# Two attention layers in fp32: where the reciprocals are issued, where the bias is added, and when the left factors are made

## The chip, the cores and the metric

The kernel runs on one core of a Trainium2 chip. A core has five engines that run side by side, each in its own order: TensorE (PE in the profile; PEld is its weight load), VectorE (DVE), ScalarE (ACT), GpSimd (POOL) and SyncE (SP), which here issues the transfers. The metric is the time of the core on the device in microseconds, as the median of three runs; lower is better.

## The reference, cut to what matters

Two attention blocks follow each other on eight images of 512 channels and 32 x 32 = 1024 tokens, all in fp32. The second has the same computation with 32 groups instead of 8.

```python
# x: (8, 512, 32, 32); C = 512, 8 heads of 64, N = 1024
xn = group_norm(x) * gn_scale + gn_bias            # 8 groups, then 32
q, k, v = split(einsum('oc,bcn->bon', qkv_w, xn) + qkv_b)
attn = softmax(einsum('bhdi,bhdj->bhij', q, k) / 8)
out = einsum('bhij,bhdj->bhdi', attn, v)
x = einsum('oc,bcn->bon', proj_w, out) + proj_b + x
```

## The kernel before

A unit is one layer of one image; there are 16, numbered from 0. Each runs through Q, K, V, the projection of the unit before it, and then attention. Products of 512 x 512 with 512 x 1024 are done by a scheme of seven half-size products with sums of factors (Winograd's form of Strassen's), and in Q, K and the projection some of the seven are cut into seven once more ("inner products"). So sums of left factors (weights) and right factors (activations) have to be made, and sums of results behind the products. In Q and K the order of the seven products is 1, 6, 2, 7, 5, 4, 3; those of INNER = (2, 5, 4, 3) are inner ones from unit 1 on.

```python
# pools (cut): ppool holds 4 tiles (exp tiles p, residual x, u3 of the first unit), accpool 2,
# trpool 2, tmppool 1, rbpool 1, tpool 1 of each tag, wpool 1 of each tag

    def blocks(name, left, right, tokens, c11, others, done, u3, inner=None, rests=None,
               rests_in=None):
        # bx, by, bz, sbank[1]: the four pairs of PSUM banks
        bx, by, bz = apair[0], sbank[0], apair[1]
        sums, taken = [], []
        ... # products(bank, k, start, stop): factor k of seven, added into bank
        def inner_products(bank, k, one, two, first=False):
            # a product cut once more into seven of half the size; three quarters end in
            # bank, the rest is copied by ScalarE into the tile "rest"
            ...
            product(1, one, True, False)
            nc.scalar.copy(rest[:, 0, :FD2], one)
            product(2, bank[:, 0, :FD2], first, True)
            product(3, bank[:, 0, FD2:], False, True)
            product(6, one, False, False)
            nc.scalar.copy(rest[:, 0, FD2:], one)
            product(5, two, True, True)
            nc.scalar.copy(rest[:, 1, FD2:], two)
            product(4, bank[:, 1, :FD2], first, True)
            product(7, one, False, True)
            taken.append(nc.scalar.copy(rest[:, 1, :FD2], one))
            return rest
        def add_rest(r, h, rest):
            if rest is not None:
                add = nc.gpsimd.tensor_add
                add(rest[:, 0, FD2:], rest[:, 0, FD2:], rest[:, 1, FD2:])
                add(rest[:, 1, FD2:], rest[:, 1, :FD2], rest[:, 1, FD2:])
                rests(r, h, rest)

        ...
        products(bx, 1, True, False)
        p1 = work(accpool, "acc", "p1")
        nc.scalar.copy(p1, bx)
        done(sums)
        products(by, 6, True, False)
        u2 = work(trpool, "tr", "u2")
        nc.vector.tensor_add(u2, by, p1)
        done(sums)
        rest = inner_products(bx, 2, sbank[1], bz)
        c11(bx)
        add_rest(0, 0, rest)
        done(sums)
        products(by, 7, False, False)
        if isinstance(u3, tuple):
            u3 = work(*u3, "u3")
        else:
            sums.append(u3)
        nc.vector.tensor_add(u3, by, p1)
        done(sums)
        twice = inner_products(bz, 5, sbank[1], bx, True)
        others(1, 1, bz, u3, twice)
        add_rest(1, 1, twice)
        done(sums)
        rest = inner_products(by, 4, bx, sbank[1])
        others(1, 0, by, p1)
        add_rest(1, 0, rest)
        done(sums)
        rest = inner_products(bz, 3, sbank[1], bx)
        others(0, 1, bz, u2, twice)
        add_rest(0, 1, rest)
        if twice is not None:
            rests(0, 1, twice)
        done(sums)
        return taken[-1:]
    def projections(w, rest):
        ...
        # done(_) counts the products of Q, K and V from 1 to 21 and runs the parts in rest[count]
        for sel, bias in (("q", QB), ("k", KB)):
            ...
            def others(r, h, bank, more, part=None):
                for i in range(2):
                    pr = 2 * r + i
                    n = FD if part is None or i == 0 else FD2
                    w.last[sel].append(
                        nc.vector.scalar_tensor_tensor(
                            tiles[pr][:, h * FD : h * FD + n], bank[:, i, :n],
                            vec[:, l, bias, pr : pr + 1], more[:, i, :n], ALU.add, ALU.add,
                        )
                    )
                if part is not None:
                    w.last[sel].append(
                        nc.scalar.activation(
                            tiles[pr][:, h * FD + FD2 : (h + 1) * FD], more[:, 1, FD2:],
                            AF.Identity, bias=vec[:, l, bias, pr : pr + 1],
                        )
                    )
            def rests(r, h, rest):
                for i in range(2):
                    cols = tiles[2 * r + i][:, ts(h, FD)]
                    w.last[sel].append(nc.gpsimd.tensor_add(cols, cols, rest[:, i, :]))

            ...
    # the projection behind attention: same blocks(); its results are stored by SyncE
    # inside attention
        def reciprocals(pr):
            def work(name):
                return small.tile([BL, 2 * BL], F32, tag=name, name=f"{name}_{u}_{pr}", bufs=1)
            lt = state["lt"]
            one, two, tot, rows, rec = map(work, ("one", "two", "tot", "rows", "rec"))
            nc.vector.tensor_add(
                one, state["red"][:BL].rearrange("i j h f -> i (j h f)"), lt[:, 0, :]
            )
            nc.vector.tensor_add(two, lt[:, 1, :], lt[:, 2, :])
            nc.vector.tensor_add(tot, one, two)
            nc.vector.transpose(rows, tot)
            nc.vector.reciprocal(rec, rows)
            ok = okay[:BL]
            nc.vector.scalar_tensor_tensor(ok, tot, SUM_MAX, ok, ALU.is_le, ALU.mult)
            nc.vector.scalar_tensor_tensor(ok, tot, SUM_MIN, ok, ALU.is_ge, ALU.mult)
            drec = dram.tile([2, N], F32, tag="drec", name=f"drec_{u}_{pr}")
            ... # rec goes to DRAM and back as rb, spread over the partitions, for divide(pr)
        ...
        parts = {4: [lambda: reciprocals(CC - 1)], 10: [divide_last], 17: mixing[:2], 18: mixing[2:3],
                 19: mixing[3:]}
    # left factors of the inner products, made once in each layer
    def mix_inner_left(l, lefts, ks, dst):
        sub = nc.gpsimd.tensor_sub
        def part(n, i, after):
            left = lefts[i][ks[n]]
            t = tpool.tile([P, 2, FD], F32, tag=("o1", "o2", "o4")[n % 3], name=f"l{i}{n}_{l}")
            s1, s2, s4 = (t[:, 0, j * P : (j + 1) * P] for j in range(3))
            a11, a12 = left[:, 0, :P], left[:, 1, :P]
            a21, a22 = left[:, 0, P:], left[:, 1, P:]
            first = nc.gpsimd.tensor_add(s1, a21, a22)
            first = getattr(first, "ins", first)
            tc.add_manual_dep(first, name_of(after), DEP, reason="spread over attention")
            sub(s2, s1, a11)
            sub(a21, a11, a21)
            sub(s4, a12, s2)
            nc.sync.dma_start(dst[l][:, i, n], t[:, 0, : 3 * P].rearrange("p (s o) -> p s o", s=3))
        return [partial(part, n, i) for n in range(len(ks)) for i in range(len(lefts))]

    # main loop over 16 units (2 layers x 8 images), cut
        left_parts = []
        if u == 0:
            left_parts = mix_inner_left(0, lefts[:2], INNER, inner_left)
        elif u == B - 1:
            left_v, mixing_w = mix_weights(1, load_weights(1, (2,)), nc.vector, 2)
            lefts = coming[0] + left_v
            left_parts = [lambda _, i=i: [part() for part in mixing_w[i : i + 2]] for i in (0, 2)]
            left_parts += mix_inner_left(1, lefts[:2], INNER, inner_left)
        elif u in (1, B + 1):
            left_parts = mix_inner_left(units[u][0], [left_o], INNER_O, inner_left_o)
            # in a step of attention (8 chunks of 8 steps):
            if left_parts and t in (3, 7) and s >= (3 + late) * NT - 1:
                left_parts.pop(0)(state["exp"][-1])
```

Of the kernel before, what the change touches and what calls it, by code (L numbers as in the profile page):

```python
# [11 lines left out]
F32 = mybir.dt.float32  # L12
# [6 lines left out]
P = 128  # L19
# [13 lines left out]
def fast_path(ctx, tc, x, qkv_wT, proj_wT, vecs, groups, out, flag):  # L33
# [184 lines left out]
    def mix_inner_left(l, lefts, ks, dst):  # L218


        sub = nc.gpsimd.tensor_sub

        def part(n, i, after):
            left = lefts[i][ks[n]]
            t = tpool.tile([P, 2, FD], F32, tag=("o1", "o2", "o4")[n % 3], name=f"l{i}{n}_{l}")
            s1, s2, s4 = (t[:, 0, j * P : (j + 1) * P] for j in range(3))
            a11, a12 = left[:, 0, :P], left[:, 1, :P]
            a21, a22 = left[:, 0, P:], left[:, 1, P:]
            first = nc.gpsimd.tensor_add(s1, a21, a22)
            first = getattr(first, "ins", first)  # L230
            tc.add_manual_dep(first, name_of(after), DEP, reason="spread over attention")
            sub(s2, s1, a11)
            sub(a21, a11, a21)
            sub(s4, a12, s2)
            nc.sync.dma_start(dst[l][:, i, n], t[:, 0, : 3 * P].rearrange("p (s o) -> p s o", s=3))

        return [partial(part, n, i) for n in range(len(ks)) for i in range(len(lefts))]

# [116 lines left out]
    def blocks(name, left, right, tokens, c11, others, done, u3, inner=None, rests=None,  # L355
               rests_in=None):
# [53 lines left out]
        def add_rest(r, h, rest):  # L410
            if rest is not None:
                add = nc.gpsimd.tensor_add
                add(rest[:, 0, FD2:], rest[:, 0, FD2:], rest[:, 1, FD2:])
                add(rest[:, 1, FD2:], rest[:, 1, :FD2], rest[:, 1, FD2:])
                rests(r, h, rest)
# [11 lines left out]
        nc.vector.tensor_add(u2, by, p1)  # L427
# [10 lines left out]
        nc.vector.tensor_add(u3, by, p1)  # L438
# [3 lines left out]
        add_rest(1, 1, twice)  # L442
# [7 lines left out]
        add_rest(0, 1, rest)  # L450
# [3 lines left out]
        return taken[-1:]  # L454

    def projections(w, rest):
# [13 lines left out]
        for sel, bias in (("q", QB), ("k", KB)):  # L470
# [12 lines left out]

            def others(r, h, bank, more, part=None):

                for i in range(2):
                    pr = 2 * r + i
                    n = FD if part is None or i == 0 else FD2
                    w.last[sel].append(
                        nc.vector.scalar_tensor_tensor(  # L490
                            tiles[pr][:, h * FD : h * FD + n], bank[:, i, :n],
                            vec[:, l, bias, pr : pr + 1], more[:, i, :n], ALU.add, ALU.add,
                        )
                    )
                if part is not None:
                    w.last[sel].append(
                        nc.scalar.activation(
                            tiles[pr][:, h * FD + FD2 : (h + 1) * FD], more[:, 1, FD2:],
                            AF.Identity, bias=vec[:, l, bias, pr : pr + 1],
                        )  # L500
                    )

            def rests(r, h, rest):
                for i in range(2):
                    cols = tiles[2 * r + i][:, ts(h, FD)]
                    w.last[sel].append(nc.gpsimd.tensor_add(cols, cols, rest[:, i, :]))  # L506
# [3 lines left out]
            if w.inner:  # L510
# [5 lines left out]
                f"{sel}_{u}", left, w.right, False, c11, others, done, u3, inner, rests,  # L516
                {
# [21 lines left out]
        blocks(f"v_{u}", w.lefts[2], w.right, True, v11, v_others, done, (ppool, "p"))  # L539

    def project(w, after):
# [47 lines left out]
        def rests(r, h, rest):  # L589
            for i in range(2):  # L590
                o = 2 * r + i
                cols = results[o, h]
                nc.gpsimd.tensor_add(cols, cols, rest[:, i, :])
                store(o, h)
# [3 lines left out]
            f"o_{w.u}", w.left, w.right_o, False, c11, others, done, (rbpool, "rb"), w.inner_o, rests,  # L598
# [29 lines left out]
    def attention(w, at_step, at_end):  # L628
# [193 lines left out]
        parts = {4: [lambda: reciprocals(CC - 1)], 10: [divide_last], 17: mixing[:2], 18: mixing[2:3],  # L822
# [51 lines left out]
    for u in range(2 * B):  # L874
# [14 lines left out]
        if u == B - 1:  # L889
# [8 lines left out]
            for i in range(2):  # L898
                rest.setdefault(20 + i, []).append(partial(mix_coming, i))
        projections(w, rest)  # L900
# [13 lines left out]
        if u == 0:  # L914
            left_parts = mix_inner_left(0, lefts[:2], INNER, inner_left)
        elif u == B - 1:
            left_v, mixing_w = mix_weights(1, load_weights(1, (2,)), nc.vector, 2)
            lefts = coming[0] + left_v
            left_parts = [lambda _, i=i: [part() for part in mixing_w[i : i + 2]] for i in (0, 2)]
            left_parts += mix_inner_left(1, lefts[:2], INNER, inner_left)  # L920
        elif u in (1, B + 1):
            left_parts = mix_inner_left(units[u][0], [left_o], INNER_O, inner_left_o)
# [5 lines left out]
        if old is not None:  # L928
# [4 lines left out]
            project(old, lambda g: stats_of(*stats_after.get(g, ())))  # L933
# [53 lines left out]
    project_last(old, [part for g in (4, 10) for part in rest[g]] + [verdict])  # L987
# [265 lines left out]
```

## Time and profile before

| | |
|---|---|
| time, median of 3 | 3295.59 us (3292.41 to 3295.63) |
| span of the profiled run | 3293.9 us, TensorE clock 0.999 |
| one unit, from Q's first product to the next unit's | about 203 us (409.0 to 612.2) |
| ... of it Q, K, V and the projection | about 93 us (409.0 to 501.9) |
| POOL's adds of 128x512 in Q, L506 | 150, mean 1366 ns |
| VectorE's sum of exp tiles, L708 | 768, mean 1259 ns |

The profile is one execution recorded by the hardware. Its page gives the busy time of each engine, the chain of work that ended last, and groups of equal instructions by source line. The trace behind it answers closer questions: the list of waits says which engine stood before which line, for whom, how long in total and how often; the timeline lists instructions in order of time. In a line such as "PE L393 MATMUL s<-xn,s4w 128*128 128x256 f32 x2" the parts are engine, source line, operation, tile written and tiles read, shape, and how many records are merged. An idle time ahead of an instruction stands in square brackets with the one that ended it.

### The profile page before, as it was taken

What the parts mean: (1) busy time and instruction counts of PE and PEld (TensorE: products, weight loads), DVE (VectorE), ACT (ScalarE), POOL (GpSimd) and SP (SyncE); (2) the same over time, 40 slices, a digit from 0 to 9 for tenths busy, and PEclk for the clock granted to TensorE, in tenths of its full rate; (3) what the DMA queues carried; (4) which work ended last, traced back from release to release, by engine and by line L of the source; (5) the groups of instructions that cost most, each with busy time, mean ns of one, the idle gap of its engine ahead of it and who ended that gap; (6) DMA issues with size and microseconds to landing.
All of it is one profiled execution on the core that took longest, in us unless ns stands there. A gap on an engine that the chain in (4) does not pass through costs nothing.

```text
span 3293.9 us, 55690 instructions
## 1 busy us (share of the span) xinstructions
PE 3259.4 (99%) x21956; PEld 1805.8 (55%) x21956; DVE 2465.0 (75%) x2989; ACT 1648.3 (50%) x2245; POOL 1208.4 (37%) x1200
## 2 busy tenths in 40 slices
PE   8999999999999999999999999999999999999999
PEld 4455474554746547465474645646556464464643
DVE  4876958769586795868958679586795967859577
ACT  1552726536265462744637436374463735637354
POOL 0171171541716317062570603706226072350710
PEclk9999999999999999999999999999999999999999
DMA  2112120121201212022121111201212012120121
GB/s 79 39 60 72 33 84 30 46 78 41 78 28 40 78 41 84 21 66 91 60 84 34 53 61 46 91 15 40 84 42 84 15 40 84 47 78 15 60 77 48
DMA packets 78105, 185.17 MB, mean 56 GB/s; under 512 B 22032, under 2 KB 26768, under 8 KB 77840
## 3 DMA queue, kind: packets, MB, share of 16 engines
q1 hardware_dynamic: 77840, 181.54, 16.2%
q8 instruction: 178, 2.92, 0.4%
q14 instruction: 87, 0.71, 0.1%
HBM read 141.52 MB, written 38.40 MB: 55 GB/s over the span
## 4 chain that ended last, share of the span: by engine, by line
PE 95%; DVE 4%; issue 1%; DMA 0%; ACT 0%; POOL 0%; SPq 0%; DVEq 0%; ACTq 0%
PE a L689 26%; PE s L661 25%; PE s L375 15%; PE a L375 14%; PE a L393 7%; PE s L393 5%; PE a L661 1%; DVE two L751 1%; DVE tot L752 1%; DVE q L490 0%; PE s L609 0%; PE a L609 0%; DVE acc L708 0%; DVE one L748 0%; DVE okay L757 0%
## 5 line engine op out<-in xcount | busy, mean ns | idle before, releaser
L669 ACT ACTIVATE p<-s 128x1024 f32<-128x1024 f32 x976 | 997.0, 1023 | 563.3 <-PE s L661 528.2
L689 PE MATMUL a<-p,v 64*64 64x512 f32 x8192 | 1097.2, 590 | 2.7 <-ACT p L669 2.5
L661 PE MATMUL s<-q,k 64*64 64x512 f32 x7808 | 1055.2, 590 | 1.4 <-DVE v L534 1.4
L708 DVE TENSOR_TENSOR acc<-acc,p 128x1024 f32<-128x1024 f32 x768 | 966.9, 1259 | 75.2 <-ACT p L669 21.6
L689 PEld LDWEIGHTS a<-p,v 64*64 64x64 f32 x8192 | 379.0, 131 | 503.5 <-ACT p L669 354.5
L661 PEld LDWEIGHTS s<-q,k 64*64 64x64 f32 x7808 | 376.6, 133 | 441.5 <-issue 432.9
L884 POOL TENSOR_TENSOR r<-xn 128x256 f32<-128x256 f32 x30 | 51.6, 1720 | 993.2 <-DVE acc L708 813.2
L300 POOL TENSOR_TENSOR y<-var,half 128x4 f32<-128x4 f32 x16 | 31.2, 1949 | 500.2 <-DVE var L298 500.2
L506 POOL TENSOR_TENSOR q<-q,m_q 128x512 f32<-128x512 f32 x150 | 201.1, 1366 | 0.0
L506 POOL TENSOR_TENSOR k<-k,m_k 128x512 f32<-128x512 f32 x150 | 186.6, 1270 | 0.0
L706 DVE TENSOR_TENSOR acc<-p,p 128x1024 f32<-128x1024 f32 x128 | 156.2, 1220 | 18.9 <-ACT p L669 18.9
L721 DVE STREAM_TRANSPOSE tr<-acc 128x1024 f32<-128x1024 f32 x128 | 157.9, 1233 | 0.0
L731 DVE TENSOR_REDUCE red<-tr 128x32 f32<-128x1024 f32 x128 | 153.9, 1202 | 0.6
L715 DVE TENSOR_TENSOR ao<-a,tmp 128x512 f32<-128x512 f32 x128 | 87.9, 687 | 65.8 <-ACT tmp L714 65.8
L423 ACT COPY p_o<-a 128x1024 f32<-128x1024 f32 x15 | 15.2, 1012 | 242.6 <-PE a L375 242.6
L375 PE MATMUL a<-xn,w 128*128 128x512 f32 x272 | 125.9, 606 | 4.0 <-DVE xn L328 4.0
L375 PE MATMUL s<-xn,w 128*128 128x512 f32 x256 | 115.2, 592 | 1.7 <-DVE xn L172 1.7
L375 PE MATMUL a<-w,xn 128*128 128x256 f32 x512 | 115.7, 379 | 0.0
L375 PE MATMUL s<-x_t,s2w 128*128 128x512 f32 x256 | 115.1, 592 | 0.0
L375 PEld LDWEIGHTS a<-w,xn 128*128 128x128 f32 x512 | 97.3, 190 | 13.7 <-issue 0.5
L771 DVE SCALAR_TENSOR_TENSOR ao<-ao,rb 128x1024 f32<-128x1024 f32 x64 | 99.6, 1556 | 6.4 <-DMA rb<-drec 6.3
L322 ACT ACTIVATE xn<-xn,shift,scale 128x512 f32<-128x512 f32 x124 | 99.4, 804 | 6.7 <-DVE shift L318 6.7
(269 smaller groups left out, 4551.5 us busy)
## 6 DMA issues: line engine op xcount, KB each, us to landing
rb<-drec SPq DMA_DIRECT2D x128, 256.0 KB, 3.9
il<-il SPq DMA_DIRECT2D x30, 768.0 KB, 5.3
xn<-mid SPq DMA_DIRECT2D x36, 512.0 KB, 7.5
xn<-x_dram SPq DMA_DIRECT2D x32, 512.0 KB, 6.9
x<-x_dram SPq DMA_DIRECT2D x32, 512.0 KB, 4.7
x<-mid SPq DMA_DIRECT2D x28, 512.0 KB, 4.7
mid<-u_o SPq DMA_DIRECT2D x32, 256.0 KB, 2.0
out_dram<-u_o SPq DMA_DIRECT2D x28, 256.0 KB, 2.1
```

Source lines behind the costliest of these rows:

```text
L322: nc.scalar.activation(cols, cols, AF.Identity, bias=st["shift"][:, c : c + 1], scale=st["scale"][:, c : c + 1],)
L375: nc.tensor.matmul(dst, at[:, c, ts(i, P)], moving[:, c, :], start=start and c == 0 and not (tokens and i % 2), stop=stop and c == 1, skip ...
L393: nc.tensor.matmul(dst, left[j], right[j], start=start, stop=stop, skip_group_check=True)
L506: w.last[sel].append(nc.gpsimd.tensor_add(cols, cols, rest[:, i, :]))
L661: nc.tensor.matmul(bank[e * H : (e + 1) * H, j, :], w.k[pr][j * H : (j + 1) * H, t * P + e * H : t * P + (e + 1) * H], w.q[pr][j * H : (j ...
L669: exp = nc.scalar.activation(p, bank, AF.Exp, scale=SCALE)
L689: nc.tensor.matmul(banks[r][j * H : (j + 1) * H, :], w.v[rows, t, lo : lo + D], p[rows, j, :], start=(t == 0), stop=(t == NT - 1),)
L706: nc.vector.tensor_add(acc, state["first"], p)
L708: nc.vector.tensor_add(acc, acc, p)
L721: nc.vector.transpose(tr, state["acc"].pop(c))
L731: nc.vector.tensor_reduce(red[:, :, qh, :], state["tr"].rearrange("p j (f i) -> p j f i", i=BL), AX.X, ALU.add)
L771: nc.vector.scalar_tensor_tensor(w.ao[pr // 2][:, pr % 2, :], w.ao[pr // 2][:, pr % 2, :], 1.0, state["rb"], ALU.mult, ALU.mult, accum_out ...
```

## The change

It has three parts. (Hunks that only pass an argument on are left out of the diff.) The reciprocals of the last pair of heads of the unit before (seven small operations of VectorE behind a transfer, for the softmax's division) are issued behind the third product of Q, not behind the fourth. The bias of Q and K is added where the two sums u2 and u3 are built, for the right half of the tokens, so that the take of the result is a plain add there and ScalarE's separate bias pass over a quarter tile (which an inner product leaves unwritten in PSUM) isn't needed; GpSimd adds the rest to the sum directly. And the sums of left factors for the inner products, which GpSimd makes once for each layer and spread over an attention stage, are made in V's stage of the first unit for layer 0, and in the projection's stage of unit 7 for layer 1, in buffers that are free there: V's weights' buffers in unit 7, for which V's own new weights are loaded later.

```diff
--- before.py
+++ after.py
@@ -220,21 +220,26 @@
 
         sub = nc.gpsimd.tensor_sub
 
-        def part(n, i, after):
+        def part(n, i, room, after=None):
             left = lefts[i][ks[n]]
-            t = tpool.tile([P, 2, FD], F32, tag=("o1", "o2", "o4")[n % 3], name=f"l{i}{n}_{l}")
-            s1, s2, s4 = (t[:, 0, j * P : (j + 1) * P] for j in range(3))
+            s1, s2, s4 = (room[:, j * P : (j + 1) * P] for j in range(3))
             a11, a12 = left[:, 0, :P], left[:, 1, :P]
             a21, a22 = left[:, 0, P:], left[:, 1, P:]
             first = nc.gpsimd.tensor_add(s1, a21, a22)
             first = getattr(first, "ins", first)
-            tc.add_manual_dep(first, name_of(after), DEP, reason="spread over attention")
+            if after is not None:
+                tc.add_manual_dep(first, name_of(after), DEP, reason="spread over attention")
             sub(s2, s1, a11)
             sub(a21, a11, a21)
             sub(s4, a12, s2)
-            nc.sync.dma_start(dst[l][:, i, n], t[:, 0, : 3 * P].rearrange("p (s o) -> p s o", s=3))
+            nc.sync.dma_start(dst[l][:, i, n], room.rearrange("p (s o) -> p s o", s=3))
 
         return [partial(part, n, i) for n in range(len(ks)) for i in range(len(lefts))]
+
+    def left_rooms(name, pool, tag, cols):
+
+        t = pool.tile([P, cols], F32, tag=tag, name=name)
+        return [t[:, i : i + 3 * P] for i in range(0, cols - 3 * P + 1, 3 * P)]
 
     def load_inner_left(u):
 
@@ -407,12 +412,13 @@
... (add_rest takes alone=None and hands it on to rests)
@@ -424,7 +430,7 @@
         done(sums)
         products(by, 6, True, False)
         u2 = work(trpool, "tr", "u2")
-        nc.vector.tensor_add(u2, by, p1)
+        summed(0, u2, by, p1)
         done(sums)
         rest = inner_products(bx, 2, sbank[1], bz)
         c11(bx)
@@ -435,11 +441,11 @@
             u3 = work(*u3, "u3")
         else:
             sums.append(u3)
-        nc.vector.tensor_add(u3, by, p1)
+        summed(1, u3, by, p1)
         done(sums)
         twice = inner_products(bz, 5, sbank[1], bx, True)
         others(1, 1, bz, u3, twice)
-        add_rest(1, 1, twice)
+        add_rest(1, 1, twice, u3)
         done(sums)
         rest = inner_products(by, 4, bx, sbank[1])
         others(1, 0, by, p1)
@@ -447,11 +453,14 @@
         done(sums)
         rest = inner_products(bz, 3, sbank[1], bx)
         others(0, 1, bz, u2, twice)
-        add_rest(0, 1, rest)
+        add_rest(0, 1, rest, u2 if twice is not None else None)
         if twice is not None:
             rests(0, 1, twice)
         done(sums)
         return taken[-1:]
+
+    def plain_sum(_, to, bank, more):
+        nc.vector.tensor_add(to, bank, more)
 
     def projections(w, rest):
 
@@ -481,29 +490,36 @@
                         )
                     )
 
+            def summed(r, to, bank, more):
+                for i in range(2):
+                    pr = 2 * r + i
+                    nc.vector.scalar_tensor_tensor(
+                        to[:, i, :], bank[:, i, :], vec[:, l, bias, pr : pr + 1], more[:, i, :],
+                        ALU.add, ALU.add,
+                    )
+
             def others(r, h, bank, more, part=None):
 
                 for i in range(2):
                     pr = 2 * r + i
                     n = FD if part is None or i == 0 else FD2
+                    to, one, two = tiles[pr][:, h * FD : h * FD + n], bank[:, i, :n], more[:, i, :n]
                     w.last[sel].append(
+                        nc.vector.tensor_add(to, one, two) if h else
                         nc.vector.scalar_tensor_tensor(
-                            tiles[pr][:, h * FD : h * FD + n], bank[:, i, :n],
-                            vec[:, l, bias, pr : pr + 1], more[:, i, :n], ALU.add, ALU.add,
+                            to, one, vec[:, l, bias, pr : pr + 1], two, ALU.add, ALU.add
                         )
                     )
-                if part is not None:
-                    w.last[sel].append(
-                        nc.scalar.activation(
-                            tiles[pr][:, h * FD + FD2 : (h + 1) * FD], more[:, 1, FD2:],
-                            AF.Identity, bias=vec[:, l, bias, pr : pr + 1],
-                        )
-                    )
-
-            def rests(r, h, rest):
+
+            def rests(r, h, rest, alone=None):
+                add = nc.gpsimd.tensor_add
                 for i in range(2):
                     cols = tiles[2 * r + i][:, ts(h, FD)]
-                    w.last[sel].append(nc.gpsimd.tensor_add(cols, cols, rest[:, i, :]))
+                    if alone is not None and i == 1:
+                        add(cols[:, FD2:], alone[:, 1, FD2:], rest[:, 1, FD2:])
+                        w.last[sel].append(add(cols[:, :FD2], cols[:, :FD2], rest[:, 1, :FD2]))
+                    else:
+                        w.last[sel].append(add(cols, cols, rest[:, i, :]))
 
@@ -536,7 +552,7 @@
... (V and the projection are given plain_sum; the projection's rests takes one argument more and ignores it)
@@ -819,7 +835,7 @@
 
         w.right_o, mixing = mix_right(f"o_{u}", *w.ao)
         w.inner_o = None
-        parts = {4: [lambda: reciprocals(CC - 1)], 10: [divide_last], 17: mixing[:2], 18: mixing[2:3],
+        parts = {3: [lambda: reciprocals(CC - 1)], 10: [divide_last], 17: mixing[:2], 18: mixing[2:3],
                  19: mixing[3:]}
         if u in (0, B):
             return parts
@@ -897,6 +913,12 @@
             rest[15].append(lambda: coming.extend(mix_weights(1, load_weights(1, (0, 1)), nc.vector)))
             for i in range(2):
                 rest.setdefault(20 + i, []).append(partial(mix_coming, i))
+        if u == 0:
+            def first_left_parts():
+                for i, part in enumerate(mix_inner_left(0, lefts[:2], INNER, inner_left)):
+                    part(left_rooms(f"l{i}", tpool, ("o1", "o2", "o4")[i % 3], 2 * FD)[0])
+
+            rest[15] = [first_left_parts]
         projections(w, rest)
         if old is not None:
             old.res = load_res(old.u)
@@ -911,15 +933,25 @@
             w.res = [again[:, c, :] for c in range(CC)]
             w.wproj = load_proj(1, "w0")
         left_parts = []
-        if u == 0:
-            left_parts = mix_inner_left(0, lefts[:2], INNER, inner_left)
-        elif u == B - 1:
-            left_v, mixing_w = mix_weights(1, load_weights(1, (2,)), nc.vector, 2)
-            lefts = coming[0] + left_v
-            left_parts = [lambda _, i=i: [part() for part in mixing_w[i : i + 2]] for i in (0, 2)]
-            left_parts += mix_inner_left(1, lefts[:2], INNER, inner_left)
+        if u == B - 1:
+
+            lefts = coming[0]
+            rooms = left_rooms("lw2", wpool, "w2", CC * C)
+            for k in (1, 2, 4):
+                rooms += left_rooms(f"ls{k}", wpool, f"s{k}w2", 2 * FD2)
+            made_parts = [
+                partial(part, room)
+                for part, room in zip(mix_inner_left(1, lefts, INNER, inner_left), rooms)
+            ]
         elif u in (1, B + 1):
-            left_parts = mix_inner_left(units[u][0], [left_o], INNER_O, inner_left_o)
+            left_parts = [
+                lambda step, i=i, part=part: part(
+                    left_rooms(f"lo{i}_{u}", tpool, f"o{i}", 2 * FD)[0], step
+                )
+                for i, part in zip(
+                    (1, 2, 4), mix_inner_left(units[u][0], [left_o], INNER_O, inner_left_o)
+                )
+            ]
 
         def stats_of(*which):
             for i in which if nxt is not None else ():
@@ -930,7 +962,20 @@
             if old.inner_o is not None:
                 old.finish()
             stats_after = {3: (0, 1, 2), 4: (3,), 6: (4, 5), 7: (6, 7)}
-            project(old, lambda g: stats_of(*stats_after.get(g, ())))
+
+            def after(g):
+                stats_of(*stats_after.get(g, ()))
+                if u == B - 1:
+                    for part in {1: made_parts[:6], 3: made_parts[6:]}.get(g, ()):
+                        part()
+
+            project(old, after)
+            if u == B - 1:
+                left_v, mixing_w = mix_weights(1, load_weights(1, (2,)), nc.vector, 2)
+                lefts = lefts + left_v
+                left_parts = [
+                    lambda _, i=i: [part() for part in mixing_w[i : i + 2]] for i in (0, 2)
+                ]
             w.evac_before, w.taken_before = old.evac, old.taken
             if old.u == B - 1:
                 (left_o,), mixing_o = mix_weights(1, [load_proj(1, "wproj")], nc.vector, 3)
@@ -984,7 +1029,7 @@
         nc.vector.tensor_reduce(low[:, 1:2], okay, AX.X, ALU.min)
         nc.vector.tensor_mul(both, low[:, 0:1], low[:, 1:2])
 
-    project_last(old, [part for g in (4, 10) for part in rest[g]] + [verdict])
+    project_last(old, [part for g in (3, 10) for part in rest[g]] + [verdict])
     nc.tensor.matmul(turns[0][:1, :1], both, ones[:, :1], start=True, stop=True)
     nc.scalar.copy(flag, turns[0][:1, :1])
 

```

## The prediction

> **What bounds the kernel now.** I read the page's first part, the chain that ended last, the list of waits, and then the timeline of one Q stage (the unit that begins its attention at 502 us), because the change is aimed there.
>
> The page, first part and the chain's summary:
> ```profile
> PE 3259.4 (99%) x21956; PEld 1805.8 (55%) x21956; DVE 2465.0 (75%) x2989; ACT 1648.3 (50%) x2245; POOL 1208.4 (37%) x1200
> PE 95%; DVE 4%; issue 1%; DMA 0%; ACT 0%; POOL 0%; SPq 0%; DVEq 0%; ACTq 0%
> ```
> TensorE is busy in all but 34.5 us of 3293.9. The change removes no matmul, so it can win only time in which TensorE stands, and some of that hides in the busy time: a matmul that starts late lengthens the row before it. The 4% of VectorE in the chain (some 130 us) is no saving of that size: the chain went back through work that ran beside a busy TensorE. What counts is the wait at its end, in the list of waits:
> ```profile
> PEld a L393 <- DVE q L490: 11.1, 14, 0.8
> PE a L393 <- DVE q L490: 5.5, 14, 0.4
> ```
> In 14 units TensorE stood for a take of Q by VectorE. The timeline shows one case (start us, duration us, engine, line):
> ```profile
> 422.68 1.23 DVE L438 TENSOR_TENSOR il<-s,p_q 128x1024 f32<-128x1024 f32 x1 [2.84 <-PE s L375]
> 423.82 0.71 DVE L748 TENSOR_TENSOR one<-red,lt 32x64 f32<-32x64 f32 x1
> 424.41 2.49 POOL L506 TENSOR_TENSOR q<-q,m_q 128x512 f32<-128x512 f32 x2
> 424.46 1.30 DVE L751 TENSOR_TENSOR two<-lt 32x64 f32<-32x64 f32 x1
> 425.79 1.20 DVE L752 TENSOR_TENSOR tot<-one,two 32x64 f32<-32x64 f32 x1
> 425.96 0.51 ACT L497 ACTIVATE q<-il,vec 128x256 f32<-128x256 f32 x1
> 426.36 0.59 PE L393 MATMUL s<-x_t,il 128*128 128x256 f32 x2
> 426.38 0.36 ACT L398 COPY m_q<-a 128x256 f32<-128x256 f32 x1
> 426.88 0.67 PE L393 MATMUL a<-r,il 128*128 128x256 f32 x2
> 427.39 0.59 PE L393 MATMUL s<-r,il 128*128 128x256 f32 x2
> 427.94 0.63 DVE L757 SCALAR_TENSOR_TENSOR okay<-tot,okay 32x64 f32<-32x64 f32 x1
> 428.50 1.12 DVE L490 SCALAR_TENSOR_TENSOR q<-a,vec,il 128x512 f32<-128x512 f32 x2
> 428.68 0.59 PE L393 MATMUL s<-xn,s4w 128*128 128x256 f32 x2
> 429.67 0.70 PE L393 MATMUL a<-xn,s4w 128*128 128x256 f32 x2 [0.40 <-DVE q L490]
> 430.21 0.59 PE L393 MATMUL a<-xn,il 128*128 128x256 f32 x2
> ```
> Three things stand here. Pairs of 128x256 matmuls normally follow each other by 0.43 us (the timeline goes on from 430.21 with 430.64 and 431.07); 428.68 to 429.67 is 0.99, so 0.56 us are lost, and the pair itself takes 0.54 before 430.21, another 0.11. Second, VectorE waited 2.84 us for TensorE (419.84 to 422.68) and only then began the reciprocals, which held the take of Q from 425.2, when its bank was full (the pair at 424.63 ended), to 428.50. Third, ScalarE's bias pass L497 keeps its copy L398 waiting, and TensorE needs that copy: 426.36 to 426.88 is 0.09 too long, 426.88 to 427.39 is 0.08.
>
> **What the Trainium skill says.** "SBUF — State Buffer", section "Who interferes with whom": a VectorE instruction with two SBUF inputs contends with a GpSimd instruction that reads SBUF, and the loser blocks for the whole instruction; one with at most one SBUF input outside the two-port modes does not. The trace agrees: L751 ends at 425.76, with the first of the two POOL adds of 1.25 us, and takes 1.30 us, while beside an idle POOL (193.15 us) it takes 0.20. Takes out of a PSUM bank keep 1.21 to 1.23 us beside POOL. "Perfetto Trace Analysis", section "Identifying the Most-Contended Engine", warns that TensorE's busy share is no measure of headroom because of pipelining; here the spacing of matmuls, not the 99%, showed the 0.56 us. [...]
>
> **The change part by part.**
> 1. Reciprocals one product earlier. Their seven small operations move from behind the sum u3 (L438) to before it, into the idle 2.84 us. Are their inputs there? The three lt transfers are issued from 416.47 on and land by 419.44 (unit at 409 us), VectorE is free at 419.84. Cost there: beside POOL adds of 0.72 us (L468) rather than 1.25 I estimate 0.2 + 0.74 + 0.74 for the sums, then 0.23, 0.54, 0.45 and 0.6: 3.5 us instead of 4.7. They end at 423.5, so u3 ends at about 424.9 instead of 423.91. Its bank is rewritten by the pair at 425.93, so 1.0 us is left. The take of Q then starts at once when its bank is full (425.2) instead of 428.50, three us before it is needed. Gain: 14 x (0.56 + 0.11) = 9.4 us.
> 2. Bias into the sums. u2 and u3 of Q and K turn from one 128x1024 operation (1.22 us) into two 128x512 with a scalar (1.39 us for two, row L490): +0.17, hidden. Takes with h = 1 turn from scalar_tensor_tensor to tensor_tensor, both about 0.65 us a piece. ScalarE loses L497: four in each of 15 units, 60 x 0.51 = 31 us of an engine that is half idle. What reaches TensorE is the late copy: 0.17 us in each Q stage and, in K (450.00 to 450.54 instead of 0.43), 0.11: 15 x 0.28 = 4.2 us; I count 3.5. POOL gets 60 more operations, since four adds a unit are cut in halves: about +0.1 us each, beside other work.
> 3. Left factors. Unit 0: 8 parts of four 128x128 operations leave its attention, where VectorE was full, for V's stage, where POOL does nothing at all. In attention one such operation took 0.45 to 1.57 us by contention. Behind it VectorE was late for Q of the next unit: matmul L375 waited 1.72 us at 215.2 for L172. I count 1.0 of that, because part of that lag is the extra mix in this unit's last chunk. Unit 7: the 8 parts (32 operations, 24.7 us of POOL between 1572 and 1629) made VectorE and then ScalarE late:
> ```profile
> 1623.09 1.57 POOL L234 TENSOR_TENSOR l<-s4w,l 128x128 f32<-128x128 f32 x1
> 1624.43 1.94 ACT L669 ACTIVATE p<-s 128x1024 f32<-128x1024 f32 x2 [3.66 <-DVE acc L706]
> 1625.60 1.98 PE L689 MATMUL a<-p,v 64*64 64x512 f32 x8 [2.47 <-ACT p L669]
> ```
> By the spacing of matmuls between 1622 and 1629, and 0.3 us at 1581, that is 4.1 us in all, which go.
> The other side: in unit 7's projection POOL is idle from 1496.4 to 1504.4 and for 5.85 us before 1514.4. Six parts ahead of its first add are 24 operations: some eight beside VectorE's mixing of the new weights at about 1.0 us, sixteen at 0.43 plus small gaps, so to about 1510 instead of 1504.4. The first rests then end at 1514 instead of 1508.5. The second product's copy L398 at 1512.19 writes the same buffer (tmp, one buffer) and so waits some 2 us, and TensorE with it. I charge 2.0 us. The sums at the start of the attention need p1's store, perhaps 1 us later than before; four p tiles cover that.
> Sum: 9.4 + 3.5 + 1.0 + 4.1 - 2.0 = 16.0. For lt transfers that land late (in the unit at 1632 and others 0.6 us after VectorE is free, and a landing can slip by 1.5) I take off 1.5: 14.5 us, 0.44%. 3295.6 - 14.5 = 3281.
>
> **The rivals.**
> A. The wait moves to u3. If the reciprocals, ahead of it, take 4.7 us as now, u3 ends at 426.1 and the pair at 425.93 waits for it, 0.3 to 0.7 us in each of 15 units. For it: every small sum can be blocked by a POOL add. Against: POOL runs its short adds then. It would leave 3287 to 3290.
> B. POOL becomes the bound in unit 7: if the parts contend throughout, at 1.0 us, six last to 1521 and the projection stalls 5 to 9 us, then the attention's start too. For it: the in-place order on POOL and the single tmp buffer. Against: most of VectorE's work in a projection is out of PSUM or with one scalar, and the POOL adds there ran at their short time (0.73). It would leave about 3287.
> C. Nothing moves: the time in which TensorE stood is filled by a later wait in the same stage. Against: K, the same code without reciprocals, shows no wait for a take. It would leave 3290 to 3295.
>
> **Range and chances.** TensorE's matmuls alone set a floor: all excess spacing in the trace sums to 37.5 us, of which some 8 lie in the first 22 us and 6 in attention steps that the change doesn't touch. So more than 25 us can't come, and 2% (66 us) is out of reach; a loss of 2% would need a stall of 4 us in every unit, of which no sign exists. Range 3274 to 3289: all gains and no stall in unit 7, or A and B in part. The three runs of before spread over 3.2 us.
>
> **What would show it.** Right: the row "PE a L393 <- DVE q" gone from the waits; one, two, tot in the gap ahead of u3 and shorter than 1.2 us; in Q the pairs 0.43 us apart through the third and fourth inner products; no L497; no 3.66 us wait of ScalarE near 1624. Wrong: a new wait of PE on u3 (s bank, fourth product of Q), or on ACT m_o in the projection before the attention at 1518, or VectorE's acc waiting for a transfer there.

## The result and the profile after

| | before | after |
|---|---|---|
| time, median of 4 | 3294.21 us | 3281.99 us (3281.50 to 3283.53) |
| ratio after to before | | 0.9964, 95% interval 0.9947 to 0.9981 |
| span of the profiled run | 3293.9 us | 3280.4 us |
| spacing of matmuls beyond the undisturbed one, summed | 37.5 us | 24.0 us |

The last row is worked out from the trace, over all matmuls in order of time: the distance from one to the next, less what it is where nothing disturbs (429 ns for 128x512, 216 for 128x256, 107 for 64x512). It fell by 13.5 us, as did the span. So the whole gain is time in which TensorE stood, began late or ran at half speed. Such half-speed stretches, in which TensorE is granted half of its clock for some microseconds, follow some of its stalls and not others (the last section has more). The profile of before has one in unit 7's attention, 1625.2 to 1628.6 us, which cost 1.5 us; the one of after has none there. That is one reason to trust the medians more than the two profiles: they fell by 12.2 us.

The page after, first part and the chain's summary:
```profile
PE 3250.3 (99%) x21956; PEld 1817.2 (55%) x21956; DVE 2448.9 (75%) x3053; ACT 1627.6 (50%) x2185; POOL 1191.1 (36%) x1260
PE 98%; DVE 1%; POOL 0%; DMA 0%; issue 0%; SPq 0%; ACT 0%; POOLq 0%
```
The counts are those foreseen: 64 instructions more on VectorE, 60 fewer on ScalarE, 60 more on GpSimd (POOL), as many matmuls. VectorE's 4% of the chain is down to 1%, but the time fell by 0.4%: most of that share was never a saving to be had. The list of waits, TensorE's rows (us in total, times, longest us), in the kernel after:
```profile
PE a L285 <- DVE mv L277: 11.3, 1, 11.3
PE a L380 <- DVE xn L333: 4.4, 1, 4.4
PE a L398 <- ACT m_o L403: 3.2, 1, 3.2
PE s L380 <- DVE xn L172: 1.8, 1, 1.8
PE s L677 <- DVE v L550: 1.4, 1, 1.4
PE a L285 <- DVE e L298: 0.9, 1, 0.9
```
The row "PE a L393 <- DVE q", 14 waits, has no successor. The third row is new: one wait, in the projection of unit 7. The fourth, in unit 1, is as it was (1.7 us before). The timeline of the same Q stage as in the prediction, now at 420 us:
```profile
420.41 0.20 DVE L764 TENSOR_TENSOR one<-red,lt 32x64 f32<-32x64 f32 x1
420.54 0.21 DVE L767 TENSOR_TENSOR two<-lt 32x64 f32<-32x64 f32 x1
420.78 0.74 DVE L768 TENSOR_TENSOR tot<-one,two 32x64 f32<-32x64 f32 x1
...
422.48 0.62 DVE L773 SCALAR_TENSOR_TENSOR okay<-tot,okay 32x64 f32<-32x64 f32 x1
...
423.15 1.41 DVE L496 SCALAR_TENSOR_TENSOR il<-s,vec,p_q 128x512 f32<-128x512 f32 x2
...
425.74 1.02 DVE L508 TENSOR_TENSOR q<-a,il 128x512 f32<-128x512 f32 x2 [1.18 <-PE a L398]
...
426.40 0.59 PE L398 MATMUL s<-x_t,w 128*128 128x256 f32 x2
...
427.26 0.59 PE L398 MATMUL a<-r,il 128*128 128x256 f32 x2
427.69 0.59 PE L398 MATMUL s<-r,il 128*128 128x256 f32 x2
...
428.99 0.59 PE L398 MATMUL s<-xn,s4w 128*128 128x256 f32 x2
429.42 0.59 PE L398 MATMUL a<-xn,s4w 128*128 128x256 f32 x2
```
The reciprocals lie in what was VectorE's idle gap. They last 2.7 us in all, not 4.7: the first two sums begin before GpSimd's next add (at 420.72 us) and take 0.2 us each. The sum u3 (il, L496) ends at 424.56, and its bank is rewritten from 426.40. The take of Q (L508) now waits for TensorE, not TensorE for the take, and the pairs are 0.43 us apart throughout.

In unit 7 the stall of the attention is gone: ScalarE's longest wait for VectorE's acc there is 0.97 us (at 1620 us), not 3.66. In its place stands this, in the projection ahead of it:
```profile
1507.89 2.93 POOL L609 TENSOR_TENSOR x<-x,m_o 128x512 f32<-128x512 f32 x2
1510.85 0.37 ACT L403 COPY m_o<-a 128x256 f32<-128x256 f32 x1 [10.49 <-POOL x L609]
1511.28 0.70 PE L398 MATMUL a<-ro,lo 128*128 128x256 f32 x2 [3.16 <-ACT m_o L403]
```
ScalarE's copy had to wait for GpSimd to leave the one tmp buffer, and TensorE for the copy: 3.33 us by the spacing.

### The profile page after: what moved, and what is told of

Read it like the earlier page. It is cut to its first block, busy times and chain, and to the rows that moved or that the text cites. A ratio compares the mean times of both kernels' runs of the same rounds, so it can differ in the third digit from the quotient of the medians.

```text
span 3280.4 us, 55764 instructions
## 1 busy us (share of the span) xinstructions
PE 3250.3 (99%) x21956; PEld 1817.2 (55%) x21956; DVE 2448.9 (75%) x3053; ACT 1627.6 (50%) x2185; POOL 1191.1 (36%) x1260
## 4 chain that ended last, share of the span: by engine, by line
PE 98%; DVE 1%; POOL 0%; DMA 0%; issue 0%; SPq 0%; ACT 0%; POOLq 0%
PE a L705 27%; PE s L677 26%; PE s L380 15%; PE a L380 14%; PE a L398 8%; PE s L398 7%; PE a L677 1%; PE s L625 0%; PE a L625 0%; DMA xn<-x_dram 0%; DVE v L550 0%; POOL x L609 0%; PE a L285 0%; POOL lw L234 0%; DVE s4w L911 0%
## 5 line engine op out<-in xcount | busy, mean ns | idle before, releaser
L522 POOL TENSOR_TENSOR k<-k,m_k 128x512 f32<-128x512 f32 x120 | 164.4, 1386 | 0.0
L522 POOL TENSOR_TENSOR q<-q,m_q 128x512 f32<-128x512 f32 x120 | 150.3, 1268 | 0.0
L463 DVE TENSOR_TENSOR u_v<-s,p_v 128x1024 f32<-128x1024 f32 x32 | 39.2, 1225 | 125.5 <-PE s L380 125.5
L463 DVE TENSOR_TENSOR u_o<-s,p_o 128x1024 f32<-128x1024 f32 x30 | 36.7, 1225 | 90.4 <-PE s L380 90.4
```

The costliest lines, as they stand in the source:

```text
L463: nc.vector.tensor_add(to, bank, more)
L522: w.last[sel].append(add(cols, cols, rest[:, i, :]))
```

## The experiments

Every ratio is to the kernel before, run on the same chip in the same group of runs; its median was 3294.2 to 3296.3 us from group to group, so ratios compare better than times.

**Each part alone.** Three kernels, each the kernel before with the hunks of one part of the diff and no others.

Part one, the reciprocals:
```diff
-        parts = {4: [lambda: reciprocals(CC - 1)], 10: [divide_last], ...
+        parts = {3: [lambda: reciprocals(CC - 1)], 10: [divide_last], ...
```


> The kernel before with the first part alone: reciprocals behind Q's third product. Theory: the late take of Q cost 14 waits of 0.56 us and 14 restarts of 0.10, so 9.2 us go and nothing comes: 3285 us beside 3294.2, ratio 0.997, and no wait of PE for a take of Q. ScalarE's bias pass still delays its copy, so the 4 us of part two stay. Rival: the gain needs part two as well, because the take with a bias (scalar_tensor_tensor) is the slow one; then waits of 0.2 us or more stay in most units and less than 5 us go.

Measured: 3286.61 us, ratio 0.9972 (0.9961 to 0.9983). All 14 waits for a take of Q are gone, and the late copies of part two stand as before (4.1 us). So the theory holds; a take without bias isn't needed for it. In the profile the span fell by 8.7 us. Half-speed stretches blur it: one behind unit 1's stall cost 1.7 us here, and the one in unit 7's attention (1.5 us) is missing.

Part two, the bias (`summed`, `others`, `rests` and `add_rest` of the diff).

> The kernel before with the second part alone: bias in the sums, ScalarE's pass gone. Theory: ScalarE's copy comes in time for the sixth inner product, which wins 0.17 us in Q and 0.10 in K in 15 units, 4.1 us: 3290 us beside 3294.2, ratio 0.9988; the wait for the take of Q stays at 0.4 us in 14 units. Rival one: nothing, because the reciprocals' wait in the same stage takes it up (0 in Q, 1.6 us from K). Rival two: the take of Q as a plain add is faster and shortens the wait too, by more than 2 us over all units.

Measured: 3295.97 us, ratio 1.0001 (0.9993 to 1.0010): nothing. The theory missed and the first rival came near. The late copies are gone (4.1 us), but TensorE now arrives sooner at a take that VectorE gives no sooner. The list of waits of this kernel:
```profile
PE a L393 <- DVE q L503: 8.6, 14, 0.6
```
It was 5.5 us before. By spacing these waits grew from 7.7 to 10.8 us, so that 1.0 us of the 4.1 was left, and 1.7 us went to a half-speed stretch in unit 1.

Part three, the left factors (`mix_inner_left`, `left_rooms` and the main loop).

> The kernel before with the third part alone: left factors in V's stage and in the projection of unit 7. Theory: in unit 7 the stalls of the attention (4.1 us) go and one of 3.4 us comes in the projection, so under 1 us is won: 3293.5 beside 3294.2, ratio 0.9998. Rival: it wins more, 2 us and above, because GpSimd's work in attention also delayed stages behind it that the other two parts hide in the full change.

Measured: 3294.52 us, ratio 0.9997 (0.9989 to 1.0006). No difference that this measurement can see, as the theory had it: the 4.5 us lost in unit 7's attention go (1.5 of them the half-speed stretch), and 3.3 us come in the projection, with 1.4 us of another such stretch behind them. (Three of the 14 waits for the take of Q are missing in this profile, some 2 us. In unit 8, one of the three, the second of the reciprocals' sums took 0.77 us in place of 1.30; why wasn't found out.)

**Parts one and two together.** The line of part one, changed in the kernel with part two.

> Parts one and two without part three. Alone, part two won nothing while its copies came in time: TensorE reached the take of Q earlier and waited there longer (10.8 us in place of 7.7). Theory: with part one that wait is gone, so part two is now worth its full 4.1 us: 4 us below the 3286.6 of part one alone, 3282 to 3283, ratio 0.9960 to the kernel before. Rival: it wins nothing here either, 3286, and the 4 us in the full change come from part three.

Measured: 3282.81 us, ratio 0.9965 (0.9952 to 0.9978). The profile has none of the late copies (4.1 us) and no wait for a take. The times alone show less: beside part one alone the median is 3.8 us lower and the ratio 0.0007 (2.3 us), and the two intervals overlap. What part two is worth rests on the spacing and on the restoration below. With part three the ratio is 0.9964: part three as it stands adds nothing that can be measured.

**What part two removes.** ScalarE's pass was put back at its place in the changed kernel, first as a copy:
```diff
+                if part is not None:
+                    nc.scalar.copy(tiles[pr][:, h * FD + FD2 : (h + 1) * FD], more[:, 1, FD2:])
```


> The changed kernel with a ScalarE copy put back where its bias pass stood (same place in the order, same size, its result is overwritten later by GpSimd's add). Theory: the 4.1 us of part two come from ScalarE's order alone, its copy for the sixth inner product standing behind this pass; then all of it comes back: 3286 us, and pairs of 0.52 and 0.51 in Q, 0.54 in K instead of 0.43. Rival: the gain came from the takes being plain adds; then 3282 stays.

Measured: 3283.99 us, ratio 0.9967 (0.9953 to 0.9981). In the profile only 1.3 us came back where I had expected 4.1: one pair in Q is 0.51 us apart where the pass had made two late (0.52 and 0.51), and the one in K is all but undisturbed. (Another 3.0 us are a half-speed stretch in unit 7.) The copy takes 0.41 us here, the bias pass took 0.51, and that tenth of a microsecond decides. So the pass was put back exactly, in the kernel with the spread parts below, which has no stall in unit 7:
```diff
+                if part is not None:
+                    nc.scalar.activation(
+                        tiles[pr][:, h * FD + FD2 : (h + 1) * FD], more[:, 1, FD2:],
+                        AF.Identity, bias=vec[:, l, bias, pr : pr + 1],
+                    )
```


> The spread kernel (3278.9) with ScalarE's bias pass put back exactly, an activation of 0.51 us (the earlier copy took 0.36); its result is overwritten by GpSimd's add. Theory: what TensorE loses is how far the pass keeps the copy behind the bank's end, so 0.15 us more in the pass bring back the 0.17 in Q and the 0.10 in K: 4.1 us, 3283. Rival: the takes as plain adds hide it, and only the 1.3 us of the copy come back: 3280.

Measured: 3282.44 us, ratio 0.9961 (0.9948 to 0.9974), beside 3278.93 and 0.9948 (0.9931 to 0.9964) without the pass. (The earlier copy took 0.41 us, not 0.36.) Its timeline in the Q stage:
```profile
426.56 0.51 ACT L514 ACTIVATE q<-il,vec 128x256 f32<-128x256 f32 x1
426.95 0.59 PE L398 MATMUL s<-x_t,il 128*128 128x256 f32 x2
426.97 0.36 ACT L403 COPY m_q<-a 128x256 f32<-128x256 f32 x1
427.47 0.67 PE L398 MATMUL a<-r,il 128*128 128x256 f32 x2
427.98 0.59 PE L398 MATMUL s<-r,il 128*128 128x256 f32 x2
```
426.95 to 427.47 is 0.52 and the next pair 0.51, the distances of the kernel before. Summed over the 30 stages of Q and K it is 4.07 us, to the hundredth what the change removed. The takes stay plain adds in this kernel, so the gain of part two is ScalarE's order alone.

**How much room is there ahead of u3?** Two or four idle operations (statistics of 512 columns, result unused) were put behind the reciprocals in the changed kernel:
```diff
+        def filler():
+            for i in range(2):  # 4 in the second kernel
+                fill = small.tile([P, 6], F32, tag="fill", name=f"fill_{u}_{i}", bufs=1)
+                nc.vector.bn_stats(fill, w.ao[0][:, 0, :FD])
-        parts = {3: [lambda: reciprocals(CC - 1)], ...
+        parts = {3: [lambda: reciprocals(CC - 1), filler], ...
```


> The changed kernel with two extra VectorE operations (statistics of 512 columns, about 0.64 us each, result unused) between the reciprocals and u3. Theory: u3 ends at 424.6 and its bank is rewritten at 426.4 (unit at 410 us), so 1.3 us more fit in the gap: 3282 us, no new wait in Q. Rival: the gap was already full and part of the change's gain is lost at u3 in many units: then 10 us more (15 units of 0.7).

> The changed kernel with four such operations, 2.6 us, ahead of u3. Theory: u3 now ends some 0.7 us behind the time at which its bank is rewritten, so TensorE waits 0.7 to 0.9 us for DVE il (u3) in 15 units: 11 to 14 us more, 3293 to 3296. Rival: VectorE's lag is absorbed elsewhere and less than 4 us are lost.

Measured: 3287.32 us, ratio 0.9978 (0.9968 to 0.9987), and 3308.53 us, ratio 1.0041 (1.0027 to 1.0056). The list of waits, first with two, then with four operations:
```profile
PE s L398 <- DVE il L496: 3.7, 7, 0.6
```
```profile
PE s L398 <- DVE il L496: 18.0, 15, 2.0
```
The room is real, but it isn't the same in each unit, and both expectations were too simple. Units 1 to 6, 14 and 15 took the two operations without a wait. Units 7 to 13 lost 0.8 us each. In units 7 to 12 of the changed kernel the lt transfers land 0.2 to 0.8 us after VectorE is free (unit 10: 2044.27 and 2043.43). The reciprocals then meet GpSimd's adds from the second sum on and last 3.9 us, not 2.7, so that u3 ends about 1.1 us later. With four operations, six units (7 to 11 and 13) lose 2.1 us each and the others 0.85, and three half-speed stretches of 1.7 us come on top. Why the transfers land later in the middle of the run wasn't found out.

**Another slot for the reciprocals.** Behind the fifth product and its take, in the changed kernel:
```diff
-        parts = {3: [lambda: reciprocals(CC - 1)], ...
+        parts = {5: [lambda: reciprocals(CC - 1)], ...
```


> The changed kernel with the reciprocals behind Q's fifth product and its take, in place of behind the third. Theory: what counts is only that they don't stand between the fourth product and the take of the fifth; any slot where the next take has slack will do. Then 3282 us as the changed kernel (within 1 us), the takes of the sixth product about 3 us later but not waited for. Rival: only the idle gap ahead of u3 is free; here they run beside GpSimd's long adds, take 4.7 us, push the takes back and TensorE waits in K or for a late division: 3 us and more.

Measured: 3280.77 us, ratio 0.9956 (0.9940 to 0.9973); the interval of the changed kernel lies over it. The take of the sixth product (L509) comes at 430.66 us, which is some 2 us later, and nobody waits for it, nor for the division at 440. So the gap ahead of u3 is one good slot and not the only one. What hurt was the slot right ahead of a take that TensorE waits for.

**The stall in unit 7.** Three, three and two parts in place of six and two:
```diff
-                    for part in {1: made_parts[:6], 3: made_parts[6:]}.get(g, ()):
+                    for part in {1: made_parts[:3], 3: made_parts[3:6], 6: made_parts[6:]}.get(g, ()):
```


> The changed kernel, with unit 7's eight left-factor parts as 3, 3 and 2 behind the first, third and sixth product of the projection, not 6 and 2. Theory: the 3.3 us stall is the second product's copy waiting for the one tmp buffer, which GpSimd frees only behind six parts; with three ahead the first rests end at about 1504.5, three us before the copy needs the buffer, and the stall goes: 3278.6 us beside 3282.0 of the changed kernel, and no wait of PE for ACT m_o. Rival: GpSimd has too much work in this stage whatever the order, and the stall moves to the start of the attention (VectorE's first sum behind p1's store), 2 to 4 us.

Measured: 3278.93 us, ratio 0.9948 (0.9931 to 0.9964). Its timeline:
```profile
1502.44 2.50 POOL L609 TENSOR_TENSOR x<-x,m_o 128x512 f32<-128x512 f32 x2
1508.12 0.37 ACT L403 COPY m_o<-a 128x256 f32<-128x256 f32 x1 [7.00 <-POOL lw L228]
1508.71 0.59 PE L398 MATMUL a<-ro,lo 128*128 128x256 f32 x2
```
The first rests leave the buffer at 1504.9, three microseconds before the copy wants it, and no PE row for ACT m_o is left. TensorE has no new wait at the start of the attention: only the order was at fault, not the amount of work. VectorE's first sum does wait there, 2.4 us (2.5 in the changed kernel), but TensorE loses nothing by it. (The name behind the copy's 7.00 us is only the last event before it. By 7.0 us that copy waits for its product in undisturbed units too.)

**The stall in unit 1.** The two sums of right factors that VectorE makes for the next unit stood in the last of eight chunks of unit 0, where other units have them one chunk earlier:
```diff
-            elif c == 2 + CC and t in (2, 5):
-                mixing[int(t == 5)]()
+            elif late and c == 1 + CC and t in (2, 7):
+                mixing[int(t == 7)]()
+            elif not late and c == 2 + CC and t in (2, 5):
+                mixing[int(t == 5)]()
```


> The changed kernel with the first two sums of right factors for unit 1 made in the seventh chunk of unit 0's attention, not in its last (other units unchanged). Theory: unit 1's 1.9 us wait for L172 comes from these two operations of 1.2 and 1.75 us in VectorE's full last chunk, not from GpSimd's left factors; moved away, it goes: 3280.0 beside 3282.0. Rival: VectorE's lag comes from GpSimd's right factors beside it at 202 to 212 us, and at least 1 us of the wait stays.

Measured: 3281.76 us, ratio 0.9959 (0.9944 to 0.9974). The wait of unit 1 fell from 1.92 to 0.09 us, so the theory of its cause holds. Yet the median is only 0.2 us below the changed kernel's. In the profile 1.7 us of half-speed stretch stand behind unit 7's stall, which were not there in the profile of the kernel after.

**Both mends.**

> The changed kernel with both mends, left-factor parts spread 3, 3, 2 and unit 1's sums one chunk earlier. If the two stalls (3.4 and 2.0 us) are apart from each other they add: 3276.7, ratio 0.9945 to the kernel before. If one hides the other, 3278.5 to 3279.

Measured: 3277.67 us (3276.28 to 3278.53), ratio 0.9947 (0.9933 to 0.9960). Both stalls are gone from its waits; spacing sums to 19.9 us. It is the fastest median of all, 4.3 us below the changed kernel, but its ratio can't be told from that of the spread parts alone (0.9948).

## Why the prediction was right

The predicted time was 3281, the measured one 3282. That is closer than the working was: a gain of 14.5 us was forecast from a median of 3295.6, and 12.2 were measured from one of 3294.2. By its own terms, in us of matmul spacing, where minus is a gain:

| step | predicted | measured |
|---|---|---|
| 1, the take of Q | -9.4 | -9.2 |
| 2, ScalarE's late copy | -3.5 | -4.1 |
| 3, unit 1's wait for L172 | -1.0 | 0.0 |
| 3, unit 7's attention | -4.1 | -4.5 (1.5 of it the half-speed stretch) |
| 3, unit 7's projection | +2.0 | +3.4 |
| late lt transfers | +1.5 | 0.0 |
| one pair in Q of unit 7 | not foreseen | +0.3 |
| unit 8's wait for L172 | not foreseen | +0.3 |

The measured terms sum to -13.8; the trace has -13.5, the rest being small differences elsewhere. The late transfers took slack from u3 in units 7 to 12 and cost TensorE nothing. The pair in Q of unit 7 isn't theirs: it waits for a right factor of GpSimd's (r, L477), and loses the same 0.3 us in the kernel that has the reciprocals behind the fifth product. Why only this unit has it wasn't found out.

Step 1 was right in mechanism and size: the part alone shows it. Its working was off. I estimated 3.5 us for the reciprocals and u3's end 1.0 us ahead of need; it is 2.7 and 1.8 us in most units. In units 7 to 12 it is about 3.9 us, and the slack is about 1.1 us less. Rival A didn't come true, but in those units it was near, as the fillers show.

Step 2 named the right operation, and the exact restoration shows it. What it didn't say is that this term hangs on step 1. The working summed the parts as if each could be had alone, while in Q the second gain runs into the first one's wait. Alone, part two won nothing.

Step 3 had two terms wrong, together 2.4 us worse than counted. Step 2, unit 7's attention and the late transfers were together 2.5 us better, which hides it: that the sum came so near was in part luck. Unit 1: "I count 1.0 of that" failed. GpSimd's left factors were not the cause of any of it: they left unit 0's attention (most of them ran from 53 to 70 us, even ahead of V's stage, and the rest before), and the wait stayed at 1.9 us. VectorE's own two sums in the last chunk were the cause, as the kernel with these moved shows (0.09 us).

Unit 7's attention: the working read all of its loss as lateness of ScalarE. About 3.0 us are that: so much the same attention loses in the profiles of part one alone and of part two alone, where no half-speed stretch follows the same stall. The other 1.5 us are the half-speed stretch, which this execution of the kernel before happened to have: the eight records at 1625.60 that the prediction shows took 1.98 us, not 1.07, at a granted clock of 0.57 between 1625 and 1629 us. (And the 24.7 us of GpSimd belong to 24 of the 32 operations; all 32 took 31.6.)

Unit 7's projection: the mechanism, one tmp buffer, was right, and the size was 3.4 instead of 2.0. I had ended the first rests at 1514 against a copy due at 1512.2, 1.8 us apart. In the kernel after, all of this lies some 4.8 us sooner: they ended at 1510.8 against a copy due at about 1507.4, 3.4 us apart. Of the 1.6 us between, about 0.8 is that the six parts took longer than estimated (they ended at 1506.0, which is 1510.8 on the time line of before, in place of 1510), and about 0.8 that the rests behind them took 4.83 us in place of 4.0: L419 1.17 instead of 0.72, L609 2.93 instead of 2.49, beside VectorE's L565.

That contention is what the Trainium skill says in "SBUF — State Buffer", "Who interferes with whom": L565 has two SBUF tensors as inputs there. It took 3.11 us for two in place of 1.41. The prediction had judged "most of VectorE's work in a projection" harmless, which these rows don't bear out.

Two of the signs of being wrong that the prediction named did appear. TensorE waited for ACT m_o in the projection (3.2 us), which its sum had charged with 2.0. And VectorE's first acc of unit 7's attention waited 2.5 us for a store (mid<-p_o), which reached nobody: TensorE's excess spacing in that attention is 0.3 us, as in the others.

## What to carry to other kernels

On an engine that is 99% busy, look for instructions that begin late, by the distance from one to the next, and follow each repeated delay back to what stands ahead of its releaser in that engine's own order; then move that, into a gap that the profile shows. Gains in one stage don't add on their own: an earlier arrival at an unmoved wait wins nothing, so the part that removes the last wait comes first. When work moves to an idle engine, set the buffer that its old work frees against the time at which the next user wants it, and spread the work around that point.

## What I had not expected of the hardware

A short stall of TensorE can cost more than itself. Behind unit 1's stall, the same eight matmul records took 3.70 us in the kernel after and 5.40 us in the kernel with part one alone:
```profile
215.97 3.70 PE L380 MATMUL s<-xn,w 128*128 128x512 f32 x8 [1.76 <-DVE xn L172]
```
```profile
216.30 5.40 PE L375 MATMUL s<-xn,w 128*128 128x512 f32 x8 [2.10 <-DVE xn L172]
```
In the second, three distances are 0.85 us in place of 0.43, and the window query gives the clock granted to TensorE (the column behind POOL's):
```profile
217.00:221.00 4.00, 4.00 (x7) 1.73 (x6) 2.79 (x8) 0.00 (x0) 3.38 (x5) 0.63 0.02 4
```
0.63 of full speed on average; the trace has half speed from 216.58 to 219.99 us, for 3.41 us. The other such stretches behind stalls are as long (twice as long, 6.83 us, behind unit 7's stall in the kernel with the copy put back), and each full one costs 1.7 us. The Trainium skill has it in "TensorE: Matmul & The Clock Gate", "What's actually happening": a gate halves the clock when a free-running window of some 3.4 us was idle. The profiles agree on the half and on 3.4 us as the length of a stretch, but stalls of 1.9 to 3.2 us were enough here. They don't always trigger it: the 3.16 us wait in the kernel after was followed by none, the 3.2 us wait of the same place in four other kernels by stretches that cost 1.4 to 3.0 us. Unit 1's stall of 1.6 to 1.8 us was followed by none in any of the nine profiles that have it at this length. Where in a window a stall falls may decide; no run here shows that. So the cost of one stall of 2 us varies from one execution to the next, and one profile doesn't tell it.
